# A graph network on one core: wider loads of edge attributes, wider stores of counts, one buffer of one-hot keys less

## The chip, the cores and the metric

The kernel runs on one core of a Trainium2 chip. The metric is the device time of one execution in microseconds (us). Before the change the median of four runs is 6497.2 us (6489.24 to 6521.17).

A core has five engines that run their own instruction streams in order and meet through semaphores: TensorE (PE in the profile; its weight loads are shown as PEld), VectorE (DVE), ScalarE (ACT), GpSimd (POOL) and SyncE (SP), which here only issues transfers. Matrix products go to PSUM, a small memory of banks; everything else lies in SBUF, 128 partitions wide. Transfers between HBM and SBUF go through 16 DMA engines, fed by the queue of SyncE and that of GpSimd.

## The reference, cut to what matters

There are 12500 nodes with 64 values each and 400000 edges, sorted by their target `dst`; `dst` is denser at low node numbers (n nodes hold a share of sqrt(n/12500) of the edges). Each edge has 32 attributes.

```python
# first layer
x_t = leaky(x @ W1n + b1n) @ W2n + b2n              # by node
e_t = leaky(edge_attr @ W1e + b1e) @ W2e + b2e      # by edge
aggregated = segment_sum(x_t[src] * e_t * dp_scale, dst)
out = layernorm(x + aggregated * res_w) * gamma + beta
x = layernorm(x + out)
# second layer, row = src and col = dst, each with a loop at every node
deg = segment_sum(1, col)
edge_weight = deg[row] ** -0.5 * deg[col] ** -0.5
h = x
for _ in range(2):
    h = segment_sum(edge_weight[:, None] * h[col], row)
x = layernorm(x + h @ W.T + b)
```

## The kernel before, in words

Four streams of work are interleaved by hand, and a scheduler then puts each engine's instructions into an order of its own.

*Quads.* The edges are cut into 261 quads of 12 x 128 edges, worked from the last to the first. `take(q)` loads a quad's attributes (`load_ea`, L612 to 615: one transfer of 192 KB on SyncE's queue, L614, into a tile `eat` of 128 x 384 numbers, out of three buffers of the pool `eap`) and starts its 12 gathers of node rows on GpSimd (L592). It is called two quads ahead. Then `hidden` multiplies the attributes (L624, TensorE; L634 on ScalarE and L638 on VectorE make the leaky step), `message` multiplies again and combines with the gathered rows (L648, L650, L659), `level1` sums 32-node pieces (L674 makes a one-hot, L684 multiplies, L693 copies the result out of PSUM), and `level2` adds it to a ring of windows of 128 nodes (L703, L713). `nodes` ends a window with its layer norms. `last_load` keeps the last load of attributes that was issued; eight zeroing transfers of 1568 KB to tables in HBM (`zero_table`, L1307, and a small one at L1312 for every second) are tied behind it, one for each of eight successive quads near the start.

*Counts.* `adjacency` (L875 on) counts edges between pairs of nodes. A block is four target nodes, there are 3125 of them, worked from the last down. For a slot of 128 edges VectorE builds a one-hot of columns, `oh` (L910, 11 buffers), and for several slots at once a one-hot of keys, `koh` (`key_onehot`, L859, pool `kohp`, 10 buffers of 128 x 512 numbers of 2 bytes); a matmul of the two (L920) counts in a PSUM bank `pa` of 128 x 391. Low blocks need many slots, high blocks one or a shared one. ScalarE copies each block's counts as 1-byte numbers into one of 8 places of a tile `stage` and sums each row for a check (L935; for the last 48 blocks VectorE takes the maximum at L932 and L933 copies). `STG = 8` is the number of places, `stgp` the pool of `stage`, with three buffers. When a chunk of 8 is full, SyncE stores it to the table `adj` in HBM (L944, 391 KB in pieces of 391 bytes), and VectorE folds the 8 sums into a check value with three small instructions (L957, L958, L961). A chunk ends early where a supergroup ends: there are ten, of 14, 14, 14, 14, 14, 12, 8, 4, 3 and 1 windows of 32 blocks from the top down, the first one short (437 blocks).

*First hop.* When a supergroup's counts are stored and its nodes are done, `hop1` loads them (L1097, L1102, three buffers `at`) and multiplies them with the node values (L1117, L1129, L1246), into `hacc`.

*Second hop.* When all blocks are counted, the pools of the counts are closed; scatter tables are made, and after the last quad the second hop runs with matmuls over the dense part (L1221, L1232) and gathers and scatter-adds for the rest (L1492), then the last layer norm.

SyncE's queue holds all of `load_ea`, the stores of counts, the zeroing transfers, the loads of the hop and the small loads and stores of `nodes`, in the scheduler's order; an instruction that waits holds back those behind it. GpSimd's queue holds the gathers; they are paced by marks on TensorE's matmuls.

The lines that the change touches directly:

```python
STG = 8
eap = main.enter_context(tc.tile_pool(name="eap", bufs=3))
kohp = counts.enter_context(tc.tile_pool(name="kohp", bufs=10))
stgp = counts.enter_context(tc.tile_pool(name="stgp", bufs=3))
```

Of the kernel before, what the change touches and what calls it, by code (L numbers as in the profile page):

```python
# [11 lines left out]
F32 = mybir.dt.float32  # L12
# [9 lines left out]
P = 128  # L22
# [10 lines left out]
SCC = 3  # L33
# [25 lines left out]
NRUN = E // ER  # L59
NCAND = 36  # L60
EXT = 130
STG = 8
MAXDUP = 16
NBIG = 48
SC = 512
# [133 lines left out]
def tile_fast(  # L199
# [42 lines left out]
    nc = tc.nc  # L242
# [29 lines left out]
    main = ExitStack()  # L272
    idxp = main.enter_context(tc.tile_pool(name="idxp", bufs=2))
    xgp = main.enter_context(tc.tile_pool(name="xgp", bufs=4))
    eap = main.enter_context(tc.tile_pool(name="eap", bufs=3))

    with tc.tile_pool(name="srch", bufs=2) as srch, tc.tile_pool(
        name="srch1", bufs=1
# [239 lines left out]
    counts = ExitStack()  # L518
    slotp = counts.enter_context(tc.tile_pool(name="slotp", bufs=1))
    slotq = counts.enter_context(tc.tile_pool(name="slotq", bufs=2))  # L520
    ohp = counts.enter_context(tc.tile_pool(name="ohp", bufs=11))
    kohp = counts.enter_context(tc.tile_pool(name="kohp", bufs=10))
    stgp = counts.enter_context(tc.tile_pool(name="stgp", bufs=3))
    psR = main.enter_context(tc.tile_pool(name="psR", bufs=1, space=PSUM))
    banks = main.enter_context(tc.tile_pool(name="banks", bufs=7, space=PSUM))

# [20 lines left out]
    xgs, eas, hs, tots = {}, {}, {}, {}  # L547
# [62 lines left out]
    last_load = [None]  # L610

    def load_ea(q):  # L612
        t = eap.tile([P, SCC * P], F32, name="eat")
        last_load[0] = nc.sync.dma_start(t, ea[q]).ins  # L614
        eas[q] = t

    def hidden(q):
        def f():
# [256 lines left out]
    def adjacency():  # L875
        i = 0
        stage = None
        for k in range(NBLK - 1, -1, -1):
# [3 lines left out]
            if stage is None:  # L882
                n = min(STG, k - lo_blk + 1)
                first = k - n + 1
                stage = stgp.tile([P, STG, FB], FP8, name="stage")
                sums = stgp.tile([P, STG], F32, name="sums")
            if w < 8:
# [406 lines left out]
    def take(q):  # L1294

        k = q // SEGQ
        if k not in seg:
            load_seg(k)
        load_ea(q)
        return gathers(q)  # L1300
# [30 lines left out]
    for t in range(NQ + 3):  # L1331
# [63 lines left out]
        if q_done is not None:  # L1395
            top = QWIN[q_done - 1][1] if q_done > 0 else -1
            while groups and groups[0][0] > top:
                lo, hi = groups.pop(0)
# [155 lines left out]
    for i, o in enumerate(ORDER):  # L1554
        with tc.high_priority(PRIO if i < 2 else 0):
            if o == "p" and prods:
                product(*prods.pop(0))
            elif o == "s" and splits:
                lo, hi = splits.pop(0)
# [755 lines left out]
def build(nc, fast, general, params, out, **kw):  # L2315
    with tile.TileContext(nc, schedule_with_timeline_sim=True) as tc, ExitStack() as ctx:
        fp = ctx.enter_context(tc.tile_pool(name="flag", bufs=1))
        flag = fp.tile([1, 1], I32, name="flag")
        tile_fast(tc, flag, *fast, *params, out, **kw)
        again = nc.values_load(flag, min_val=0, max_val=1)  # L2320
        with tc.If(again > 0):
            tile_general(
                tc, *general, *params, out.rearrange("(p j) d -> p j d", j=NJ)
            )
# [27 lines left out]
```

## Time and profile before

| what | value |
|---|---|
| median of four runs | 6497.2 us |
| the profiled execution | 6496.0 us |
| its span, from the first instruction to the last | 6494.3 us |
| mean granted clock of TensorE | 0.796 of full speed |
| copies of counts (L935), first and last start | 147.5 and 5012.0 us |
| attribute matmuls (L624), first and last start | 138.9 and 5695.5 us |
| transfers of L944 and L614 | 391 and 261 |
| their time in SyncE's queue, median of one | 360 and 346 ns |

The page gives for each engine its busy time and number of instructions. Matmul ends are modelled, so a busy TensorE isn't one at its peak. The chain that ended last is followed back from the last instruction, at each step to what released it. Groups of instructions are by line, engine and tile; after the bar stand the busy time in us, the mean of one in ns, and the engine's idle time just before them with what ended it. A row of windows has the stretch, its length, then busy us of PE, PEld, DVE, ACT and POOL with counts, the granted clock, the mean busy share of the 16 DMA engines, and GB/s. Transfers can be followed by packet: the trace has start, length and size of each, and packets of 391 bytes belong to L944 alone, those of 12544 bytes to L1307.

### The profile page before, as it was taken

The page shows a single profiled execution, that of the slowest core. Times are in us where ns is not written, and L with a number is a line of the kernel's source. Part 1 is how long each engine was busy: PE and PEld are TensorE (multiplying, and loading weights), DVE is VectorE, ACT ScalarE, POOL GpSimd, SP SyncE. Part 2 cuts the span into 40 slices and gives each one's busy share as a digit, 9 for nine tenths or more (in the row PEclk, how much of TensorE's full clock was granted, in tenths as well). Part 3 has the DMA queues.
Part 4 walks back from the last instruction along what each step waited for, and adds up shares of the span by engine and source line. Part 5 has one row for each costly group of instructions (what it writes and reads, how often), then busy time and mean ns, then how long its engine had stood idle before and what let it go on. Part 6 is the DMA issues. An engine that isn't in the chain of part 4 may idle for free.

```text
span 6494.3 us, 94143 instructions
## 1 busy us (share of the span) xinstructions
PE 4974.3 (77%) x31344; PEld 2753.5 (42%) x31344; DVE 3330.1 (51%) x11086; ACT 2268.4 (35%) x7868; POOL 3738.0 (58%) x3607
## 2 busy tenths in 40 slices
PE   4666778888887788867777677767757776599998
PEld 2333344444444444433444344434433444344444
DVE  5667666555455555555555555565655664430003
ACT  2667565444333333344333333233322111220002
POOL 4666545666555455565444555655665553448886
PEclk6777788988887787776777677878877776599999
DMA  3655555545444344423333243323322223279998
GB/s 102 144 134 119 115 122 112 119 110 118 103 108 104 82 104 100 90 66 91 92 96 84 61 102 84 89 61 93 80 53 56 57 52 98 77 175 215 208 203 215
DMA packets 1254836, 696.96 MB, mean 107 GB/s; under 512 B 593468, under 2 KB 1188144, under 8 KB 1253312
## 3 DMA queue, kind: packets, MB, share of 16 engines
q1 hardware_dynamic: 1104032, 566.91, 34.3%
q0 software_dynamic: 150304, 123.92, 11.3%
q8 instruction: 248, 4.06, 0.3%
q14 instruction: 252, 2.06, 0.1%
HBM read 494.67 MB, written 195.83 MB: 106 GB/s over the span
## 4 chain that ended last, share of the span: by engine, by line
PE 64%; another core or an unknown queue 14%; ACT 7%; issue 6%; DVE 4%; DMA 1%; POOL 1%; SPq 0%; DVEq 0%; ACTq 0%; POOLq 0%
PE pa L920 15%; PE hacc_p L1117 10%; PE pw L624 6%; PE acc L1221 6%; PE pe L650 5%; ACT stage L935 5%; PE pc L1246 5%; PE hacc_p L1129 5%; PE ring L713 3%; PE acc L1232 3%; PE pl L684 2%; PE pe L648 2%; DVE oh L910 1%; PE pk L1078 1%
## 5 line engine op out<-in xcount | busy, mean ns | idle before, releaser
L592 POOL DMA_INDIRECT xg<-xt_tab,si x3125 | 3074.8, 984 | 2488.9 <-PE pa L920 727.8
L935 ACT ACTIVATE stage<-pa 128x391 fp8e4<-128x391 f32 x3077 | 1505.1, 514 | 1485.6 <-PE pa L920 1087.1
L910 DVE TENSOR_SCALAR oh<-iota_b,colT 128x391 bf16<-128x391 bf16 x5556 | 1624.8, 334 | 663.7 <-PE pa L920 437.1
L920 PE MATMUL pa<-oh,koh 128*128 128x391 bf16 (+2 forms) x6054 | 1411.3, 405 | 261.3 <-issue 124.5
L920 PEld LDWEIGHTS <-koh 128*128 128x128 bf16 (+2 forms) x6054 | 622.4, 154 | 755.3 <-issue 508.9
L1117 PE MATMUL hacc_p<-at,gp 128*128 128x512 fp8e4 (+1 forms) x2425 | 756.0, 449 | 82.3 <-DMA at<-adj 32.8
L624 PE MATMUL pw<-eat,w1ab 64*128 64x384 f32 x1044 | 519.4, 763 | 321.7 <-ACT tot L693 244.1
L935 ACT ACTIVATION_READ_ACCUMULATOR stage<-pa 128x1 f32 x3077 | 678.4, 220 | 0.0
L674 DVE TENSOR_TENSOR oh<-iota_f,rel 128x384 f32<-128x384 f32 x261 | 145.5, 558 | 986.4 <-remote 763.0
L713 PE MATMUL ring<-tot,oh 128*128 128x65 f32 x1096 | 258.0, 381 | 405.2 <-ACT tot L693 356.5
L1492 POOL DMA_INDIRECT hop_tab<-tot,first x317 | 493.6, 1557 | 100.4 <-issue 94.6
L650 PEld LDWEIGHTS pe<-w,z 128*128 128x128 f32 x3132 | 478.1, 214 | 102.9 <-issue 82.1
L650 PE MATMUL pe<-w,z 128*128 128x128 f32 x3132 | 488.2, 297 | 5.0 <-issue 4.8
L693 ACT COPY tot<-pl 128x65 f32<-128x65 f32 x261 | 55.8, 214 | 1161.2 <-remote 811.4
L713 PEld LDWEIGHTS ring<-tot,oh 128*128 128x128 f32 x1096 | 218.5, 280 | 571.3 <-ACT tot L693 415.1
L1117 PEld LDWEIGHTS <-gp 128*128 128x128 bf16 x2425 | 259.4, 114 | 473.3 <-issue 297.3
L659 DVE TENSOR_TENSOR msg<-pe,xg 128x384 f32<-128x384 f32 x522 | 288.1, 552 | 334.8 <-PE pe L650 261.0
L1221 PE MATMUL acc<-at,gp 128*128 128x512 fp8e4 (+1 forms) x2000 | 446.3, 376 | 0.0
L1129 PE MATMUL hacc_p<-at,gp 128*64 128x512 fp8e4 (+1 forms) x2425 | 384.0, 400 | 10.2 <-issue 10.1
L859 DVE TENSOR_TENSOR koh<-iota_k,keyT 128x512 bf16<-128x512 bf16 (+3 forms) x920 | 384.9, 419 | 0.0
L634 ACT ACTIVATE z<-pw,b1s 128x384 f32<-128x384 f32 x522 | 291.0, 599 | 248.2 <-PE pw L624 156.5
L624 PEld LDWEIGHTS pw<-eat,w1ab 64*128 64x128 f32 x1044 | 167.0, 257 | 484.2 <-ACT tot L693 279.9
(218 smaller groups left out, 4339.7 us busy)
## 6 DMA issues: line engine op xcount, KB each, us to landing
adj<-stage SPq DMA_DIRECT2D x390, 391.0 KB
at<-adj SPq DMA_DIRECT2D x97, 896.0 KB
at<-adj SPq DMA_DIRECT2D x168, 512.0 KB
eat<-in_eaq_dram SPq DMA_DIRECT2D x261, 192.0 KB
xg<-xt_tab,si POOLq DMA_INDIRECT x3125
at<-adj SPq DMA_DIRECT2D x96, 256.0 KB
at<-adj SPq DMA_DIRECT2D x24, 832.0 KB
at<-adj SPq DMA_DIRECT2D x24, 768.0 KB
```

The source lines that it names most:

```text
L592: got = nc.gpsimd.indirect_dma_start(out=xg[:, i, :], out_offset=None, in_=xt_tab, in_offset=bass.IndirectOffsetOnAxis(ap=si[:, c : c + 1] ...
L624: nc.tensor.matmul(pws[h], w1ab[rows, h, :], ea_q[rows], start=True, stop=True, tile_position=(D * h, 0),)
L650: ended = nc.tensor.matmul(pe[:, :, c, :], z[:, h, c * P : (c + 1) * P], w2, start=False, stop=(c == SCC - 1),)
L713: nc.tensor.matmul(ring[:, w % RING, :], oh[:, (w - lo) * P : (w - lo + 1) * P], tot, start=False, stop=False, skip_group_check=True,)
L859: nc.vector.tensor_tensor(t[:, :, :n], iota_8[:, :, :n] if w == 8 else iota_k[:, : w * FA, :n], keyT[:, None, j0 : j0 + n].to_broadcast([P ...
L910: nc.vector.tensor_scalar(oh, iota_b, colT[:, i % P : i % P + 1], None, op0=ALU.is_equal)
L920: ended = nc.tensor.matmul(to, key, oh, start=(j == 0), stop=(j == caps[g] - 1), tile_position=(0, r0),)
L935: nc.scalar.activation(stage[:, u, :], pa, AF.Identity, saturate=True, accum_out=sums[:, u : u + 1],)
L1117: nc.tensor.matmul(acc[:, :w], gp[:kk, lo + i, 0:2, :].rearrange("p t d -> p (t d)"), t[:kk, i, :w], start=start, stop=False, skip_group_c ...
L1129: nc.tensor.matmul(acc[D * h : D * (h + 1), :w], gp[:kk, lo + i, 2, :], t[:kk, i, :w], start=False, stop=False, skip_group_check=True, til ...
L1221: nc.tensor.matmul(acc[:, :w], gp[:kk, wi, 0:2, :].rearrange("p t d -> p (t d)"), t[:kk, wi - lo, :w], start=first and n == 0, stop=False, ...
L1492: nc.gpsimd.indirect_dma_start(out=hop_tab[(q * QC + i) % HT], out_offset=bass.IndirectOffsetOnAxis(ap=first[:, q - Q0, i : i + 1], axis=0 ...
```

## The change

The attributes of two quads are loaded by one transfer of 384 KB, into one of two buffers that hold two quads each; the call for the second quad of a pair does nothing. A chunk of counts has 14 blocks instead of 8 (684 KB), and there are two buffers for chunks instead of three. The pool of key one-hots has 9 buffers instead of 10. The lines from L613 on move down by up to 7 in the changed kernel.

```diff
-STG = 8
+STG = 14
...
-    eap = main.enter_context(tc.tile_pool(name="eap", bufs=3))
+    eap = main.enter_context(tc.tile_pool(name="eap", bufs=2))
...
-    kohp = counts.enter_context(tc.tile_pool(name="kohp", bufs=10))
-    stgp = counts.enter_context(tc.tile_pool(name="stgp", bufs=3))
+    kohp = counts.enter_context(tc.tile_pool(name="kohp", bufs=9))
+    stgp = counts.enter_context(tc.tile_pool(name="stgp", bufs=2))
...
     def load_ea(q):
-        t = eap.tile([P, SCC * P], F32, name="eat")
-        last_load[0] = nc.sync.dma_start(t, ea[q]).ins
-        eas[q] = t
+
+        if q in eas:
+            return
+        lo = max(0, q - 1)
+        t = eap.tile([P, 2, SCC * P], F32, name="eat")
+        last_load[0] = nc.sync.dma_start(
+            t[:, : q - lo + 1], ea[lo : q + 1].rearrange("q p x -> p q x")
+        ).ins
+        for i in range(lo, q + 1):
+            eas[i] = t[:, i - lo]
```

## The prediction

> **What bounds the kernel now.** I read the page's busy line first, then the chain that ended last, then windows of 200 us, then the waits. Busy times and the chain (engine, busy us, share; then shares of the span):
>
> ```profile
> PE 4974.3 (77%) x31344; PEld 2753.5 (42%) x31344; DVE 3330.1 (51%) x11086; ACT 2268.4 (35%) x7868; POOL 3738.0 (58%) x3607
> ...
> PE 64%; another core or an unknown queue 14%; ACT 7%; issue 6%; DVE 4%; DMA 1%; POOL 1%; SPq 0%; DVEq 0%; ACTq 0%; POOLq 0%
> ```
>
> The reader is to see that TensorE carries the chain, that VectorE holds 4% of it (260 us of 6494.3), ScalarE 7% (455 us), transfers 1%, and the queue of SyncE, where the diff makes most of its savings, 0%. The 14% of "another core" are again TensorE: those gaps stand before the copy of L693 and before L674, and both wait only for TensorE's semaphore. Two windows, one early, one in the middle (stretch, length, busy us of PE, PEld, DVE, ACT, POOL with counts, granted clock, DMA share, GB/s):
>
> ```profile
> 200.00:400.00 200.00, 129.79 (x726) 69.57 (x727) 135.04 (x514) 136.60 (x540) 127.75 (x129) 0.74 0.67 166
> ...
> 2400.00:2600.00 200.00, 161.19 (x921) 90.43 (x921) 108.89 (x387) 73.85 (x265) 105.11 (x109) 0.76 0.43 102
> ```
>
> Early, three engines are about equally full, and ScalarE's copies of counts (L935) set the pace; in the middle TensorE does. So a stall of ScalarE counts early only, and relief of VectorE counts little anywhere.
>
> **What the change removes.** Chunks of 14 instead of 8 blocks: cutting each supergroup's blocks by 14 gives 227 stores for 391, and the built order has the same. Each chunk also has three small VectorE instructions (groups: busy us, mean ns | idle before):
>
> ```profile
> L961 DVE TENSOR_TENSOR chk<-chk,top 128x1 f32<-128x1 f32 x391 | 59.4, 152 | 3.6
> L957 DVE TENSOR_REDUCE top<-sums 128x1 f32<-128x8 f32 x390 | 58.3, 149 | 8.9 <-ACT stage L935 6.2 <-issue 2.1
> L958 DVE TENSOR_SCALAR top<-top 128x1 f32<-128x1 f32 x391 | 56.4, 144 | 3.0
> ```
>
> 164 chunks fewer x (152 + 149 + 144 ns) = 73.0 us of VectorE. Bounds: none of it or all of it. VectorE's share on the chain is 260 of 3330 busy us, 7.8%, and I take that: -5.7 us. The rest lies under TensorE, which VectorE's one-hots (L910) await for 437.1 us in the table of waits; without that cover all 73 us would show.
>
> In the built order 369 more of the one-hots (774 for 405) carry a second wait, on VectorE's own older write of the same buffer; the row of such waits gives 21 ns, 7.7 us in all, at 7.8%: +0.6 us. ScalarE loses 116 separate waits (843 for 959) at the 38 ns median of L935's row, 4.4 us; its chain share is 455 of 2268, 20%: -0.9 us. TensorE loses 110 (368 for 478), because every second quad no longer waits for a load; 51 ns in the row of L624, 5.6 us; half of it at the front of its queue: -2.8 us.
>
> SyncE issues 164 + 130 = 294 transfers fewer at about 0.36 us, 106 us of its queue. Its longest waits (us in total, times, longest):
>
> ```profile
> SPq L944 <- ACT stage L935: 1207.3, 198, 18.8
> SPq L614 <- PE pw L624: 539.1, 120, 22.8
> ...
> SPq L1097 <- DMA adj<-stage: 5.7, 2, 4.0
> ```
>
> It idles for the data that it is to move. In the same trace the stores leave 0.1 us before the chunk's last accumulator read ends in nine cases of ten, so nothing queues behind a blocked load; I cost this at 0, and what hides it is that idle time. The paired load is not later either: the single load for quad t+2 waits for L624 of quad t-1 (three buffers), and the pair for t+2 and t+3 waits for the same matmul (two buffers of two). The pair moves 384 KB for 192 KB, and its first half is still needed two quads on, some 43 us (L624 runs 261 quads from 138.9 to 5695.5 us).
>
> The Trainium skill, "SBUF — State Buffer", section on the DMA setup-cost knee, says that each transfer pays a roughly fixed 2 us and that transfers are best coalesced. By that rule alone 294 x 2 = 588 us would be an estimate of the saving. The trace lets nothing wait for it: the chain has 1% DMA, so the sum goes without it.
>
> **What it adds: a later buffer.** Before, a stage buffer is written again 16 blocks after its last copy (two other buffers of 8), now 14 blocks after (one other buffer). By the packet records a store of 391 KB alone has its first packet 0.9 us after issue and its last at 2.6; behind a zeroing table (L1307) the first came up to 5.6 us after issue and the last at 8.3. The packets are as small as before (391 bytes), so 14 blocks take 1.7 x 14/8 = 3.0 us: 3.9 us alone, 8.6 behind one table. The cover comes from the starts of the 3125 stage copies in order, cut by 14: from the end of one chunk to the start of the chunk after next there are 7.2 to 23 us before 500 us (median 11.4), and after 1000 us never under 9.3, with a median over 25. So 3.9 us is covered everywhere but once: the first supergroup has 437 = 31 x 14 + 3 blocks, and behind its chunk of 3 the old buffer is wanted after 1.15 us, at 491 us. That costs 3.9 - 1.15 = 2.7 to 8.6 - 1.15 = 7.5; I take 4, nearer the store alone.
>
> The second place is the tables. Before, each stands behind its own load, and stores come between (issue time, queue time):
>
> ```profile
> 281.88 0.85 SPq L1307 DMA_DIRECT2D hop_tab<-hacc  x1
> 282.78 0.43 SPq L1312 DMA_DIRECT2D hop_tab<-hacc  x1
> 285.60 4.18 SPq L944 DMA_DIRECT2D adj<-stage  x2
> 298.21 0.35 SPq L614 DMA_DIRECT2D eat<-in_eaq_dram  x1
> 298.61 0.42 SPq L1307 DMA_DIRECT2D hop_tab<-hacc  x1
> ```
>
> The tables are tied to the last load issued. With every second load gone, the built order has them in pairs behind one load: two of the four pairs with no store between, two with one. Their packets take 4.4 to 6.1 us a table. A store right behind a pair then lands 8.6 + 5 + 1 (the load's second half) = 14.6 us after issue, against a cover of 11.4: 3.2 us of ScalarE for two pairs, and nothing where the store comes when the tables are half through. Bounds 0 and 4 x 7 (cover 7.2); I take 6.
>
> The Trainium skill, "DMA: Bandwidth & Descriptors", section on queues, rings and completion order, says that each DMA engine consumes the descriptors of a queue in ring order; that is the rule that speaks against pairing the tables. The store of 245.6 us, 5.6 us late behind a table, agrees with it; the sum stands on that row alone.
>
> Smaller: nine key buffers. The key building (L859) stands a median of 4 one-hots later in the built order, while the one-hots are bounded by their own 11 buffers; weight loads of L920 now await keys for 14.8 us, so 0 to 15, taken at 2. A supergroup's last store is 1.3 us longer (3.9 - 2.6) before its counts can be read, nine times, 0 to 12, taken at 1, since the loads of L1097 wait only 5.7 us for stores in the whole run.
>
> **The sum.** -5.7 + 0.6 - 0.9 - 2.8 + 4 + 6 + 2 + 1 = +4.2 us. The profiled execution took 6496.0 us (span 6494.3, 1.7 us around it), 1.2 below the median 6497.2: 6500 us.
>
> **The rivals.** *The stage buffer binds* (slower). Place: ScalarE's copies before 1000 us, where the cover is 7 to 13 us. Price, from the same cut: at a landing of 7 us the shortfalls add up to 5.8 us in one chunk, at 9 us 20.7 us in 14 chunks, at 12 us 90 us in 39. It decides from a landing of about 10 us on. For it: stores of 8 blocks have taken 8.3 us next to other traffic, and the DMA share is 0.67 at 200 to 400 us. Against it: most took 2.6 to 3.3. With 90 us for the two stage terms' 10: 6580 us.
>
> *VectorE's relief counts in full* where it is as full as the others: 54 of the 164 chunks saved lie before 1000 us (127 for 73), 24 us, and if half of the other 49 us shows too, 48.5 us instead of 5.7: 6457 us. For it: VectorE has 135 of 200 us there. Against it: weight loads and matmuls of L920 wait for one-hots only 55 us in the whole run.
>
> *The change doesn't do what it says*: everything is hidden, stores included, and only the order differs by a few instructions, 6496 us. This lies inside the forecast and is counted with it.
>
> One thing can enlarge either side: the granted clock went from 0.50 to 1.00 within the two us from 282 to 284, so a new gap on TensorE can slow what follows. I widen the range for it, and shift nothing.
>
> **How the numbers follow.** A measurement here tells about 0.5% (32 us) from no change. Forecast, within 32 us: 0.47. Stage buffer binds, or gaps that add up on TensorE: 0.29. VectorE's relief shows: 0.24. All gains together (73 + 4.4 + 5.6) give 6413, all losses (7.7 + 90 + 15 + 12) 6621; neither end comes whole, and 6435 to 6590 leaves 2 in 10 outside. The forecast's own range is 6475 to 6525.
>
> **What would show it.** In the changed kernel's profile: the three small groups with 227 instructions each and VectorE near 3265 us busy; ScalarE waiting for DMA on adj only around 491 us and behind the paired tables at 240 to 400 us, some 10 us; SyncE's stores still leaving with the chunk's end; windows after 1000 us unchanged within noise. It is wrong if L935 waits for its stores again and again before 1000 us (the slower rival), if the windows up to 1000 us get shorter by 20 us and more (the faster one), or if TensorE's gaps before L713 and L624, 600.6 us behind L693, change: nothing in the diff touches them.

## The result, and the profile after

The changed kernel takes 6513.1 us (median of 40 runs, 6487.9 to 6534.1) against 6498.6 us of the kernel before beside it (66 runs, 6478.7 to 6529.1). The ratio is 1.0019 with a 95% interval of 1.0011 to 1.0027: by it 12 us more, 7 to 18. That lies within 32 us of the predicted 6500 us and inside the range, on the slow side of the forecast. The profiled execution took 6512.24 us, its span is 6510.5 us and its clock 0.797. A later run on another chip, below, shows the same change costing 102 us.

The page of the changed kernel: busy times, SyncE's queue (packets, MB, share of 16 engines' span), and the chain by engine.

```profile
PE 4969.8 (76%) x31344; PEld 2755.1 (42%) x31344; DVE 3284.8 (50%) x10594; ACT 2274.2 (35%) x7868; POOL 3746.5 (58%) x3607
...
q1 hardware_dynamic: 1099328, 566.89, 39.8%
...
PE 63%; another core or an unknown queue 14%; ACT 7%; issue 7%; DVE 4%; DMA 2%; POOL 0%; SPq 0%; DVEq 0%; POOLq 0%; ACTq 0%
```

VectorE has 492 instructions and 45.3 us less, and the chain hardly shifts: 2% of transfers for 1%. The line to look at is that of the queue. In the kernel before it was:

```profile
q1 hardware_dynamic: 1104032, 566.91, 34.3%
```

Nearly the same bytes in slightly fewer packets take 39.8% of the engines' time for 34.3%: the packets became longer.

The three small groups (busy us, mean ns | idle before) and the waits of SyncE and ScalarE (us in total, times, longest) of the changed kernel:

```profile
L964 DVE TENSOR_REDUCE top<-sums 128x1 f32<-128x14 f32 (+1 forms) x227 | 35.4, 156 | 6.4 <-ACT stage L942 4.4 <-issue 1.5
L968 DVE TENSOR_TENSOR chk<-chk,top 128x1 f32<-128x1 f32 x227 | 34.6, 153 | 2.0
L965 DVE TENSOR_SCALAR top<-top 128x1 f32<-128x1 f32 x227 | 32.9, 145 | 1.9
```

```profile
SPq L951 <- ACT stage L942: 1065.5, 120, 26.9
...
SPq L618 <- PE pw L631: 419.3, 54, 37.4
...
ACT stage L942 <- DMA adj<-stage: 14.2, 5, 6.0
```

There are 227 of each, as predicted. SyncE still idles for its data. The last line is new: ScalarE's copies now wait for stores, 14.2 us in five places. By stretch these are 3.6 us between 140 and 420 us (the tables), 6.0 between 420 and 560 us (the chunk of 3) and 4.5 after 800 us.

The windows that the prediction showed, in the changed kernel:

```profile
200.00:400.00 200.00, 128.04 (x711) 69.85 (x711) 128.65 (x453) 132.59 (x525) 121.05 (x125) 0.71 0.74 161
2400.00:2600.00 200.00, 161.69 (x906) 90.08 (x905) 106.84 (x365) 74.27 (x264) 106.58 (x110) 0.75 0.49 99
```

Early, ScalarE got through 525 instructions for 540, with the DMA engines busier (0.74 for 0.67) at fewer GB/s (161 for 166). In the middle the DMA share went from 0.43 to 0.49 as well, and TensorE's busy time stayed (161.69 us for 161.19).

SyncE's timeline at a pair of zeroing tables (start, us in the queue):

```profile
243.37 1.40 SPq L618 DMA_DIRECT2D eat<-in_eaq_dram  x1
244.81 0.48 SPq L1314 DMA_DIRECT2D hop_tab<-hacc  x1
245.35 0.42 SPq L1319 DMA_DIRECT2D hop_tab<-hacc  x1
245.82 1.07 SPq L1314 DMA_DIRECT2D hop_tab<-hacc  x1
246.98 1.20 SPq L555 DMA_DIRECT2D dn<-in_dstn_dram  x1
249.23 0.37 SPq L951 DMA_DIRECT2D adj<-stage  x1
```

By the packets of 391 bytes the store issued at 249.23 us began 7.5 us later and ended 14.2 us after its issue; the prediction had a first packet after 11.6 us and the end at 14.6.

### The profile page after: what moved, and what is told of

Its sections match the earlier page's. It is cut to its first block, busy times and chain, and to the rows that moved or that the text cites. A ratio compares the mean times of both kernels' runs of the same rounds, so it can differ in the third digit from the quotient of the medians.

```text
span 6510.5 us, 93179 instructions
## 1 busy us (share of the span) xinstructions
PE 4969.8 (76%) x31344; PEld 2755.1 (42%) x31344; DVE 3284.8 (50%) x10594; ACT 2274.2 (35%) x7868; POOL 3746.5 (58%) x3607
## 3 DMA queue, kind: packets, MB, share of 16 engines
q1 hardware_dynamic: 1099328, 566.89, 39.8%
q8 instruction: 247, 4.05, 0.3%
## 4 chain that ended last, share of the span: by engine, by line
PE 63%; another core or an unknown queue 14%; ACT 7%; issue 7%; DVE 4%; DMA 2%; POOL 0%; SPq 0%; DVEq 0%; POOLq 0%; ACTq 0%
PE pa L927 14%; PE hacc_p L1124 10%; PE pw L631 6%; PE acc L1228 6%; PE pe L657 5%; ACT stage L942 5%; PE hacc_p L1136 5%; PE pc L1253 5%; PE ring L720 3%; PE acc L1239 3%; PE pe L655 2%; PE pl L691 2%; DVE oh L917 1%; PE pk L1085 1%
## 5 line engine op out<-in xcount | busy, mean ns | idle before, releaser
L592 POOL DMA_INDIRECT xg<-xt_tab,si x3125 | 3081.7, 986 | 2493.0 <-PE pa L927 760.9
```

What stands on the lines that cost most here:

```text
L592: got = nc.gpsimd.indirect_dma_start(out=xg[:, i, :], out_offset=None, in_=xt_tab, in_offset=bass.IndirectOffsetOnAxis(ap=si[:, c : c + 1] ...
```

## The experiments

Three chips were used (the first is that of the result), and the kernel before takes 6498.6, 6608.2 and 5058 to 5063 us on them. So runs are only compared with the kernel before on the same chip.

### Second chip: the parts one by one

Kernel before 6608.2 us (35 runs).

**Chunks of 14 alone.**

```diff
-STG = 8
+STG = 14
...
-    stgp = counts.enter_context(tc.tile_pool(name="stgp", bufs=3))
+    stgp = counts.enter_context(tc.tile_pool(name="stgp", bufs=2))
```

> The kernel before with chunks of 14 blocks and two stage buffers alone; loads and key buffers as before. My theory (the loss is the paired zeroing tables and the chunk of 3 blocks): the tables are apart here, so ScalarE waits for stores under 6 us, at 490 us alone, its 380th copy (451 us before) is late by at most 2 us, and the ratio to before is 0.9995 to 1.0008. Rival, two stage buffers are too few by themselves: ScalarE waits 10 us and more, the 380th copy is 7 to 9 us late as in the changed kernel, ratio 1.0015 to 1.0025. Rival, nine key buffers: ratio 1.000, no copy late.

6622.5 us, ratio 1.0027 (1.0008 to 1.0047). ScalarE waits for stores 20.7 us in 7 places, 9.7 of them between 420 and 560 us, where the chunk of 3 lies. Stores land after 6.35 us (median) with packets of 47.0 ns. Waits and ratio are those of the rival with two stage buffers, not of my theory: without any paired tables the chunks alone cost as much as the whole change did on the first chip. The changed kernel as it stands was not run on this chip.

**Paired loads alone** (the new `load_ea`, two buffers of pairs).

> The kernel before with the paired loads alone; chunks of 8 in three buffers, ten key buffers. My theory: the tables stand in pairs, but a stage buffer has two others behind it, and stores behind a pair land late by 5 us against a slack of 3.5 to 10 us, so ScalarE waits for stores 3 us at most and the ratio is 0.9995 to 1.0005. Rival, pairing hurts by itself (loads or tables in the way of other transfers): 1.0015 to 1.0025 without a wait of ScalarE. Rival, two stage buffers: 1.000.

6620.5 us, ratio 1.0018 (1.0001 to 1.0035). ScalarE never waits for a store, and packets are short, 28.7 ns. If there is a loss (the interval all but touches 1), it isn't in the stage buffer.

**Nine key buffers alone.**

> The kernel before with nine key buffers alone. My theory: 0 to 2 us, ratio 1.000 to 1.0004, weight loads of the counts wait for keys some 15 us as before. Rival, the key buffer is the loss: ratio 1.0015 to 1.0025 and weight loads wait for keys 25 us and more.

6587.9 us, ratio 0.998 (0.996 to 1.000). Weight loads wait 15.0 us for keys. The predicted cost of 2 us does not exist; this is the smallest ratio of all runs, with an interval that touches 1, so not a version to call faster.

**The changed kernel with its tables spread**: one zeroing transfer behind each paired load, from the first pair on.

```diff
-        if 0 <= t - ZERO < 2 * HT:
+        if t % 2 == 0 and t // 2 < 2 * HT:
...
-                zero_table(t - ZERO)
+                zero_table(t // 2)
```

> The changed kernel with one zeroing transfer behind each paired load, from the first load on, instead of two; everything else as changed. My theory: ScalarE's waits for stores fall from 14.2 us to 6 or less, the 380th copy is at most 3 us later than in the kernel before (8.9 in the changed one), ratio to before 1.0003 to 1.0010. Rival, two stage buffers by themselves: waits 10 us and more, 380th copy 7 to 9 us late, ratio 1.0019 as in the changed kernel. Rival, key buffer: 380th copy late as in the changed one.

6607.8 us, ratio 0.9998 (0.9981 to 1.0015), although ScalarE still waits 20.1 us for stores in 10 places. So 20 us of such waits need not show in the time, and the parts do not add up: two of them alone cost 12 to 14 us, nearly all of the change together nothing. With intervals 22 to 26 us wide, the second chip can't divide 12 us.

### Third chip: the kernel before 22% quicker

Here the granted clock is 0.90 instead of 0.80, and the waits of the kernel before look different:

> The kernel before once more, for a trace from the same chip as the three below. All theories: ratio 1.000 within its interval, ScalarE waits for stores 0 to 6 us, packets of the stores 26 to 29 ns long.

A second copy of the kernel before: 5063.2 us, ratio 0.9996 (0.9987 to 1.0005) to 5062.8 (23 runs). That is the noise. Its packets are 32.7 ns, over the 26 to 29 expected, and so are ScalarE's waits for stores, 42.9 us for 0 to 6:

```profile
ACT stage L935 <- DMA adj<-stage: 42.9, 13, 15.0
...
DVE msg L659 <- DMA xg<-xt_tab,si: 342.0, 153, 10.0
```

Transfers bind more here: VectorE waits 342 us for gathered rows (L659), where the kernel before on the first chip waited 2.9 us. ScalarE waits for stores already with chunks of 8.

**Each chunk of the changed kernel stored in two transfers of 7**, the first as soon as its seven blocks are there.

```diff
+            half = n // 2
-            if k == first:
-                r0 = (first - lo_blk) * 4
+            if k == first or (half and k == first + half):
+                ha, hz = (0, half) if k == first else (half, n)
+                if k == first and not half:
+                    hz = n
+                r0 = (first + ha - lo_blk) * 4
...
-                    stage[:, :n, :],
+                    stage[:, ha:hz, :],
```

> The changed kernel with each chunk of 14 stored in two transfers of 7 blocks, the first as soon as its 7 are there. Chunks, buffers, loads, tables and VectorE's instructions are as changed. Theory, the long store behind two buffers is the loss (12 us): ScalarE's waits for stores fall from 14 to 20 us to 6 or less, packets are 26 to 30 ns long again (40 to 47 with 14 blocks), ratio to before 0.9995 to 1.0010. Rival, the loss is in the paired loads and tables or in the order: waits fall too, and the ratio stays at 1.0015 to 1.0025. Rival, packets are long because of two buffers and not of the size of a store: they stay at 40 ns and more.

5085.4 us, ratio 1.0046 (1.0033 to 1.0059), 10 waits for stores (47.8 us). Packets are 30.4 ns, short again with the same two buffers of 14: it is the size of one store that makes its packets long. The waits are not the 6 us or less that were expected, but about those of the kernel before on this chip.

**The kernel before with the check once per supergroup** instead of once per chunk (1143 small VectorE instructions fewer):

```diff
-                sums = stgp.tile([P, STG], F32, name="sums")
+                sums = stgp.tile([P, SGMAX * 32], F32, name="sums", bufs=1)
...
+                if k == lo_blk:
+                    top = stgp.tile([P, 1], F32, name="top")
+                    nc.vector.tensor_reduce(top, sums[:, :n_sg], AX.X, ALU.max)
...
```

> The kernel before with the check of the sums made once for a supergroup instead of once for a chunk: 3 x 381 small VectorE instructions fewer, 170 us of VectorE. My price of VectorE's relief (7.8% of it): 13 us, ratio 0.997 to 0.999. Rival, relief shows in full: 0.974 to 0.980. Rival, it is hidden altogether: 0.9995 to 1.0010, and of the changed kernel's 73 us of relief nothing is to be credited.

VectorE is busy 3174.6 us for 3270.5 (170 us less were expected), and the time is 5082.8 us, ratio 1.0040 (1.0026 to 1.0054): 96 us of relief give nothing, though VectorE is fuller on this chip (65% against 51%). The edit costs 20 us instead; whether by its new order or by the single buffer of sums isn't told apart.

**Three buffers of 10.**

> The kernel before with chunks of 10 blocks in three buffers; nothing else. VectorE has about 34 us less: 2.6 us by my price, ratio 0.9990 to 1.0000; no wait of ScalarE for stores beyond 4 us. Packets of the stores: if their length grows evenly with the blocks in a store, 31 to 33 ns; if there is a step between 8 and 14 blocks, either 26 to 29 ns or 38 and more.

5060.4 us, ratio 1.0000 (0.9989 to 1.0012), with packets of 39.3 ns, the step of the expectation and not the even growth. ScalarE waits 39.7 us for stores, where under 4 were expected and the kernel before waits 42.9. A quarter larger and in three buffers, the store costs nothing.

### Third chip again: buffer or packets

Kernel before 5057.5 us (9 runs). Four kernels: the changed one; the kernel before with chunks of 14 in two and in three stage buffers (to make room, both have six key buffers, and `top` becomes a column of `sums`); and the kernel before with two buffers of 8. The edit of the two in the middle, but for the two stage buffers of the first:

```diff
-STG = 8
+STG = 14
...
-    kohp = counts.enter_context(tc.tile_pool(name="kohp", bufs=10))
+    kohp = counts.enter_context(tc.tile_pool(name="kohp", bufs=6))
...
-                sums = stgp.tile([P, STG], F32, name="sums")
+                sums = stgp.tile([P, STG + 1], F32, name="sums", bufs=2)
...
-                top = stgp.tile([P, 1], F32, name="top")
+                top = sums[:, STG : STG + 1]
```

> The changed kernel itself, so that its cost stands beside the next three on one chip. All theories: 1.001 to 1.005 of before, if the chip runs like the first two; packets of stores some 40 ns or more on average, ScalarE waits for stores around 491 us and behind the paired tables.

> Chunks of 14 in two stage buffers, loads single, six key buffers (the control of the next run; six is where three stage buffers of 14 find room). Late-buffer theory (ScalarE waits for the older stage buffer): slower than the next run by 0.10 to 0.25%, that is 6 to 16 us, with ScalarE waits for stores of 10 us and more. Long-packet theory (stores of 14 rows keep the DMA engines longer, and gathers and loads behind them come late): as the next run within 0.1%. Order theory (any change in the interleaving of VectorE's and ScalarE's instructions costs some 10 us): as the next run within 0.1%. If six key buffers are too few, both runs are slower than before by the same amount, and weight loads wait for keys by more than 15 us.

> The same with three stage buffers of 14: a buffer is wanted again 28 blocks after its last copy, a cover of 19 to 25 us before 550 us where the store lands within 14. Late-buffer theory: ScalarE waits for no store at all, and the time is 6 to 16 us under the two-buffer run, within 0.1% of before if six key buffers cost nothing. Long-packet and order theories: no wait for a store, and still as slow as the two-buffer run within 0.1%; packets of stores stay as long as in the two-buffer run.

> The kernel before with two stage buffers instead of three, nothing else; no order of instructions changes but for the wait. The cover falls to 3.9 to 9.9 us before 550 us (median 5.7), and by the copies of the kernel before the shortfalls add up to 0.5 us at a landing of 2.6 us, 1.2 at 3.3, 11 in 23 chunks at 4.5, 60 in 55 chunks at 5.7. Late-buffer theory: ScalarE waits for stores in 20 to 60 chunks, 10 to 60 us in all, and the time is 0.15 to 0.9% over before. Long-packet and order theories: waits may show, but the time is within 0.1% of before, since a wait of ScalarE for a store is then no cause of the loss, and packets are as short as before.

| third chip | rows per store | stage buffers | packet, ns | store lands, us (median) | ScalarE waits for stores, us (times) | gather's last packet, us (90%) | VectorE waits for gathers, us | ratio (interval) | granted clock |
|---|---|---|---|---|---|---|---|---|---|
| before, again | 8 | 3 | 32.7 | 4.31 | 42.9 (13) | 4.03 | 342.0 | 0.9996 (0.9987 to 1.0005) | 0.905 |
| three of 10 | 10 | 3 | 39.3 | 5.36 | 39.7 (8) | 4.43 | 358.5 | 1.0000 (0.9989 to 1.0012) | 0.904 |
| changed, halves | 7 | 2 of 14 | 30.4 | 3.85 | 47.8 (10) | 4.05 | 367.1 | 1.0046 (1.0033 to 1.0059) | 0.904 |
| changed | 14 | 2 | 48.8 | 7.29 | 104.8 (37) | 5.51 | 412.7 | 1.0201 (1.0181 to 1.0220) | 0.895 |
| 14, two buffers, six keys | 14 | 2 | 48.9 | 7.18 | 95.9 (31) | 5.33 | 420.0 | 1.0206 (1.0187 to 1.0224) | 0.894 |
| 14, three buffers, six keys | 14 | 3 | 49.0 | 7.29 | 10.2 (6) | 5.52 | 416.1 | 1.0144 (1.0119 to 1.0170) | 0.896 |
| two of 8 | 8 | 2 | 30.7 | 4.06 | 177.4 (78) | 3.84 | 330.5 | 1.0215 (1.0195 to 1.0235) | 0.889 |

The packet column is the mean of the 391-byte packets; the gather column runs from the end of a gather's issue on GpSimd (L592) to its last 2048-byte packet; ratio and clock are over all runs of a kernel, the other figures from the one profiled run of each.

The changed kernel costs 102 us here, 2.0%: the condition of my expectation, a chip that runs like the first two, isn't met. Its waits, those of two and three buffers of 14 with six keys, and those of two buffers of 8:

```profile
ACT stage L942 <- DMA adj<-stage: 104.8, 37, 9.2
...
DVE msg L666 <- DMA xg<-xt_tab,si: 412.7, 146, 9.1
```

```profile
ACT stage L935 <- DMA adj<-stage: 95.9, 31, 10.3
```

```profile
ACT stage L935 <- DMA adj<-stage: 10.2, 6, 3.5
...
DVE msg L659 <- DMA xg<-xt_tab,si: 416.1, 145, 10.0
```

```profile
ACT stage L935 <- DMA adj<-stage: 177.4, 78, 18.4
...
DVE msg L659 <- DMA xg<-xt_tab,si: 330.5, 135, 7.8
```

The four fences are in that order. Both theories are half right. A third buffer takes ScalarE's waits from 95.9 to 10.2 us and gives back 26.5 us (5165.8 to 5139.3), as the late-buffer theory had it and more than its 16, but 82 us over the kernel before remain. Two buffers of 8 have short packets and quick gathers and lose 108 us; 78 waits and 177.4 us are more than the 20 to 60 of each expected. So a late buffer is enough to lose 2%, and long stores with a buffer to spare, in another order and with six keys, lose most of it; together, in the changed kernel, they cost no more than the late buffer of 8 alone.

TensorE's clock moved as well. The four kernels that lose over 1% have lower granted clocks than the others in the table: 0.887 to 0.900 in their single runs, against 0.904 to 0.909 in the runs of the kernel before beside them. Up to the sixty-fourth quad (L624), the kernel before, the changed one, three buffers of 14 and two of 8:

```profile
0.00:1130.00 1130.00, 900.38 (x5994) 509.85 (x5998) 869.89 (x3055) 772.68 (x2974) 834.00 (x834) 0.89 0.81 151
```

```profile
0.00:1176.00 1176.00, 921.66 (x5974) 514.44 (x5974) 848.96 (x2844) 775.77 (x2974) 838.28 (x832) 0.88 0.88 145
```

```profile
0.00:1153.00 1153.00, 885.98 (x5974) 506.88 (x5974) 844.94 (x2841) 773.73 (x2974) 825.45 (x833) 0.90 0.91 148
```

```profile
0.00:1238.00 1238.00, 966.96 (x5974) 537.65 (x5974) 877.31 (x3055) 778.69 (x2974) 830.99 (x833) 0.84 0.69 138
```

With two buffers of 8 TensorE is busy 67 us longer for the same work, at a clock of 0.84 for 0.89: of the 108 us lost here, 67 are TensorE itself and only the rest is idle time. In the changed kernel it is 21 of 46 us, with three buffers of 14 none. Nothing but the number of stage buffers differs between the kernel before and two of 8, so the buffer is the first cause; that the gaps behind its waits lowered the clock, as the prediction thought possible, fits these rows, but no run sets the clock apart.

Where the long stores cost: three buffers of 14 are 23 us late when the sixty-fourth quad is multiplied (L624), 74 us at the hundred and sixty-fourth. TensorE's waits between these two quads, kernel before and three buffers of 14:

```profile
PE pa L920 <- DVE msg L659: 45.4, 18, 14.4
PE pl L684 <- DVE msg L659: 38.0, 11, 16.4
PE hacc_p L1117 <- DMA at<-adj: 24.4, 2, 13.1
```

```profile
PE pl L684 <- DVE msg L659: 76.4, 14, 14.5
PE pa L920 <- DVE msg L659: 46.2, 22, 13.9
PE hacc_p L1117 <- DMA at<-adj: 31.1, 2, 16.0
```

TensorE awaits the messages 39.2 us longer, the loads of counts 6.7 us, and is itself busy 1403 us for 1394. That is 55 us by these rows, and the stretch is 51 us longer (1587 for 1536). Why the messages are late isn't shown in full: in this stretch VectorE awaits gathered rows 146.7 us for 132.0, but with six key buffers it also waits 28.3 us to write keys. The changed kernel, with nine, has no such wait; there VectorE awaits gathered rows 168.2 us, TensorE the messages some 27 us longer, and the stretch is 38 us longer. The gather column fits: with three buffers of 14 the first packet of a gather comes 1.97 us after its issue (mean) instead of 1.48, while gather packets are no longer than before (197 ns for 214). The longer the store, the later a gather begins.

The changed kernel and two buffers of 8 lose earlier: at the sixty-fourth quad (1130 us in the kernel before) the changed kernel is 46 us late, two buffers of 8 are 108 us late, and the latter lose nothing after that.

Three things these runs leave open. Six key buffers made VectorE wait 38 us to write keys in both kernels; beside the changed kernel with nine the time differs by 6 us, so they seem to cost little, but three buffers with nine keys have no room and were not tried. The changed kernel in halves still loses 23 us, with two buffers, paired loads and another order all in it. And the check once per supergroup loses 20 us with the stores and the stage buffers of the kernel before, so up to that much of the 82 us of three buffers of 14 may be order.

## Why the prediction was right, and where it was off

**The forecast.** Right in its class and nearly in its size: +4.2 us expected, +12 measured (7 to 18). It holds for a chip like the first; on the third the first rival happened.

**The added waits, mechanism right, size off.** The places (chunk of 3, tables) came as worked out. That the landing behind a pair did (14.2 us against 14.6) is luck: the store began earlier than predicted (7.5 us after issue for 11.6) and took longer (6.7 us for 3.0). The mis-sized term is the store: "14 blocks take 1.7 x 14/8 = 3.0 us: 3.9 us alone". The median store takes 5.74 us (4.93 at the tenth percentile, 7.83 at the ninetieth) against 2.99 for 8 blocks, because "the packets are as small as before" was true of their bytes only: they take 39.8 ns for 26.6 on average. With it the chunk of 3 costs 6.0 us of waiting for 4 predicted, within its bounds of 2.7 to 7.5. The tables show 3.6 us for 6. With 4.5 us at late chunks that weren't listed, ScalarE's waits for stores are 14.2 us against 10 in the two terms.

**VectorE's relief.** Credited with 7.8% of 73 us, -5.7. The check once per supergroup removes 96 us and the time grows by 20 us on the third chip: no run shows a share of it as gain. The three small groups went from 174.1 to 102.9 us, as costed; everything else on VectorE grew by 26 us where 8 were counted, so it stands at 3284.8 us and not 3265. Without the credit the sum would be +9.9, close to what was measured; that the credit is the missing 6 us is argued, not shown, since the experiment is another edit on another chip. The other terms of 1 to 3 us (second waits, ScalarE's and TensorE's fewer waits, a supergroup's last store) are smaller than these runs resolve.

**Key buffers, SyncE.** Nine key buffers cost nothing (0.998); 294 transfers fewer bring nothing, as costed: pairs alone are not faster (1.0018), and SyncE still idles.

**What was said to stay.** The middle did: the changed kernel is 9.5 us late at the sixty-first quad and 9.0 at the hundred and sixty-first (L624). TensorE's gaps before the ring and the attribute matmuls behind L693 are 610.3 us for 600.6.

**What isn't settled on the first chip.** The changed kernel is 13 us late after 280 of the 3125 copies (370 us in the kernel before), where ScalarE has waited some 3 us for stores. The rest of that delay has no row. One profile of each kernel and single runs that differ by 12 us (one standard deviation) don't carry a further division, and the parts measured one by one don't add up.

**The first rival, on another chip.** It named ScalarE's copies before 1000 us, "decides from a landing of about 10 us on", and priced 90 us in 39 chunks. On the third chip ScalarE waits 104.8 us in 37 places, with a median landing of only 7.3 us: the cover shrinks with the pace. From the copies of the kernel before, two buffers of 14 cover 11.2 us on the first chip (median before 550 us) and 8.1 on the third, while stores take longer there. The same subtraction gives 37 us in 32 chunks at a landing of 8 us. So the rival's point of decision was a property of one chip, and my range and chances were as well. That its 90 us, the 104.8 us of waits and the 102 us lost lie so near each other is luck: taking 86 us of these waits away with a third buffer gives back only 26.5 us. What the rival lacked is the second cost of the long store, late gathers, and the lower clock.

## What to carry to other kernels

A buffer's cover is work and a transfer is time: on a chip that works faster the cover shrinks and the landing doesn't, so a margin of 11 us against 6 is no margin for another chip, and both should be stated. When transfers are merged, look at the packets' length and at the other queue's latency, not at the number of issues: 294 issues less were worth nothing, and stores of 14 rows delayed the gathers beside them. Stored in two halves, the chunk of 14 lost 23 us where in one transfer it lost 102. If larger stores are wanted, test three buffers and a middle size (10 rows cost nothing here) before fewer buffers of a large one; no version that was run beats the kernel before by more than its interval.

## What the runs showed of the hardware

**Late packets of a long store take longer.** 391-byte packets took, on average, 30.4, 32.7, 39.3 and 48.8 ns on the third chip with 7, 8, 10 and 14 rows per partition (30.7 with 8 in another kernel), 26.6 and 39.8 ns on the first with 8 and 14. In the changed kernel 90% end within 78 ns, before within 33. Packets of 512 bytes in the same kernels stayed (32.0 and 32.5 ns). The length comes at the end of a store. In order of their starts, mean ns of each row's 128 packets in full stores:

| kernel, chip | rows 1 to 7 | row 8 | row 9 | rows 10 to 14 |
|---|---|---|---|---|
| before, first | 24.5 to 27.6 | 35.7 | | |
| changed, first | 24.0 to 25.7 | 27.7 | 38.8 | 60.4 to 67.7 |
| before, third | 27.5 to 34.9 | 54.9 | | |
| changed, third | 25.2 to 28.6 | 39.2 | 65.7 | 76.9 to 81.8 |

So a store of 14 rows goes as fast as one of 8 for its first eight rows, and its last five take two and a half to three times as long per packet. Scaling the store of 8 by 14/8, as the prediction did, can't see that. Why it is so is open.

The Trainium skill, "SBUF — State Buffer", section on the DMA setup-cost knee, fits a transfer as 2 us plus its bytes at 436 GB/s: by it stores of 8 and 14 rows (400 and 701 KB) would take 2.9 and 3.6 us as estimates. The trace of the first chip has 2.99 and 5.74: the small store agrees, the large one does not, and the measurement decides.

**Gathers wait for stores, though they are of another queue.** With no packet of SyncE's queue under way 0.7 us after the end of its issue, a gather's first packet comes after 0.71 to 0.75 us (mean; both chips, kernel before and changed). With a store under way it comes after 1.72 us on the first chip and 2.09 us on the third where the store has 8 rows, and after 2.71 and 3.45 us where it has 14. On the third chip nine of ten gathers have landed 3.8 to 4.1 us after their issue beside stores of 7 and 8 rows, 4.4 beside 10, 5.3 to 5.5 beside 14; on the first 3.1 and 4.1 beside 8 and 14, where VectorE waited only 2.9 and 7.5 us for them. The Trainium skill, "DMA: Bandwidth & Descriptors", section on queues, rings and completion order, says that a DMA engine takes turns between the queues in packets of many descriptors; a gather that waits for such a turn fits these numbers, but no run here shows the turns.

**Chips differ by more than the change.** The kernel before takes 6498.6, 6608.2 and 5062.8 us with mean granted clocks of 0.796, 0.787 and 0.904. Most visible is one wait. Kernel before on the first chip:

```profile
ACT tot L693 <- remote: 811.4, 150, 14.0
...
PE ring L713 <- ACT tot L693: 356.5, 94, 15.8
```

and on the third, where the first of these lines does not exist:

```profile
PE ring L713 <- ACT tot L693: 6.0, 15, 1.5
```

There the copies of L693 wait almost only for the matmuls of L684, 178.0 us in 95 places. And the ring's matmuls (L713) take 294 ns for 381, while those of L684 take 232 ns on both. The row of 811.4 us is 12% of the first chip's span: most of the 14% of the chain that the prediction called "again TensorE" goes with the chip as much as with the kernel. What that wait is remains open.
